# Spreading the first attention loads over the second sequence's projections, and hand-set program order through the last two attention units

## The chip, the cores and the metric

The kernel runs on one core of one Trainium2 chip. The metric is device time of one launch in microseconds (us); lower is better. The time of a kernel is the median of several runs. Engines are named as in the profile: PE is TensorE's matmul stream and PEld its weight loads, DVE is VectorE, ACT is ScalarE, POOL is GpSimd, and SP issues DMAs.

## What is computed

One transformer block in fp32, with layer norms behind each half. B=2 sequences of L=1024 tokens, D=512, 16 heads of 32. Cut to what matters:

```python
q = _split(lora_linear(x, Wq, bq, Bq, Aq))      # k and v alike
scores = jnp.einsum('bhqd,bhkd->bhqk', q, k) * SCALE
attn = jax.nn.softmax(scores, axis=-1)
out = jnp.einsum('bhqk,bhkd->bhqd', attn, v)
x = _layernorm(x + lora_linear(out, Wo, bo, Bo, Ao))
# FFN: 8 experts with 256 places each, top-1 routing, H=704
eidx = jnp.argmax(softmax(xt @ Wg), -1)          # tokens are dispatched to experts
h = silu(xd @ W1) * (xd @ W3);  oe = h @ W2
shared = silu(xt @ sw1) * (xt @ sw3) @ sw2
x = _layernorm(x + gate * oe[slot] + shared)
```

## The kernel before

**Precision.** Every large operand is split into a high and a low part (xh and xl, wh and wl, at_h and at_l, w13s's two halves), and a product takes three matmuls: high by high, low by high, high by low.

**Phase 1, projections (to L386).** Tokens go in four blocks tb of 512; tb 0 and 1 are the first sequence, tb 2 and 3 the second. For each block proj_qk (L290) runs eight times (four groups g of four heads, for q and for k), 12 matmuls each (L288) into one PSUM bank. store_qk (L298) then writes the high part oh on ACT (L303) and the low part ol on DVE (L304) into SBUF tiles of which there are two each, and SP stores both to DRAM (L305, L306; 256 KB each). Next come four proj_v (L308; L314 on PE, L319 on DVE, a store to vd at L321). The x tiles of the next block are loaded (L267) and split (xh on ACT L273, xl on DVE L274) meanwhile. During tb 3 a matmul stream for the first attention units is interleaved (pre_s1, L173): it finds row maxima (DVE, L181). Attention reads q, k and v back from DRAM in another layout: load_k (L130) is 3 DMAs of 512 KB, load_q (L152) 3 of 256 KB, load_v (L140) one of 512 KB. The loads for units 0 to 2 are issued in two blocks: k(0), q(0), q(1), k(1), q(2) after tb 1, and v(0) to v(3) after tb 2 (L378 to L386). In phase 1 only PE keeps the program's order; the order on ACT, DVE and SP is chosen by the tile scheduler. In the trace each of SP's DMAs waits for the one issued eight earlier to have landed: the store issued at 89.19 us waited for the qs load issued at 82.72, which landed at 89.13. mh and ml (L194 to L197) are the row maxima of a unit, stored as extra rows of its q tile.

**Phase 2, attention (from L543).** 16 units u (a sequence, four heads, 512 queries), eight steps of 128 keys each, 128 steps t in all. In a step, st_step (L555) makes four score matmuls (L566), each followed by an exponential on ACT (L575) that writes half of a tile pt; av_step (L590) makes the four value matmuls of the step before (L596). The softmax denominator is made by adding the pt tiles of a unit's steps (add_step, L578, the adds at L585) in two pairs pr of heads; the tables ON_DVE and DVE_END say which adds (step, pair) run on DVE, all others run on POOL. finish (L610) sums the result over partitions by matmuls with ones into sm (L619). The last step of a unit is not added but summed by four more of these matmuls (DIRECT), except in the units listed in NO_DIR. For units below RDIR=14 the inverse takes a way through DRAM (sd, r, invert at L640 with the reciprocal at L643, rd, and rb at L647); for units 14 and 15 it is one DVE reciprocal, rc (L629). normalize (L652) multiplies by the inverse (av, L658) and writes at_h on ACT (L660) and at_l on DVE (L662). oproj (L673) is the output projection of 128 tokens: 12 matmuls (L687), the residual add on DVE (L692), norm statistics (L529 to L532), the root on POOL (L538, L540) and the normalised row on ACT (L544). I write op10 to op17 for those of the second sequence. op10 is a generator of four times three matmuls that the loop advances once a step from step t = 128 + OPROJ1 on; what is left runs after the loop.

**What sets the order.** In the loop (L707 to L755) all engines keep the program's order (MAN2) until t = 112 (MAN_END); there steps.close() hands ACT, DVE, POOL and SP back to the scheduler, and only PE stays in program order.

**The tail (L756 on).** After the loop: op11 to op13, the router's setup (L418), and then the list TAIL in PE's order: normalize(15) ("n"), the splits of the shared expert's weight chunks w13 (s0 to s5: high on ACT at L509, low on POOL at L515, loads w13r on SP into two buffers at L501), transposes (p, L411, with xth on ACT L414 and xtl on DVE L415), op14 to op17 (o), logits (a, L464). Then follow the shared expert (L810), routing, dispatch and the experts.

Of the kernel before, what the change touches and what calls it, by code (L numbers as in the profile page):

```python
# [10 lines left out]
F32R = mybir.dt.float32r  # L11
# [7 lines left out]
P = 128  # L19
B, L, D = 2, 1024, 512  # L20
NU = 16
T = B * L
NH, HD = 16, 32
NG = 4
# [11 lines left out]
WARM, WCOL = 4, 256  # L36
OPER = 4
PTB = 13
MAN1 = {mybir.EngineType.PE}
MAN2 = {  # L40
    mybir.EngineType.PE, mybir.EngineType.Activation, mybir.EngineType.DVE,
# [2 lines left out]
MAN3 = {mybir.EngineType.PE}  # L44
MAN4 = MAN2 - MAN3
DIRECT = (7,)
MAN_END = 14 * 8
NO_DIR = (NU - 2, NU - 1)
FIN = 3
REC = 4  # L50
XTB = 5
# [11 lines left out]
FINE, NRME = 2, 4  # L63
DVE_END = {
    NU - 2: ((1, 0), (2, 1), (4, 1), (5, 1), (6, 0), (6, 1), (7, 0), (7, 1)),
    NU - 1: ((1, 0), (2, 0), (3, 0), (4, 0), (5, 0), (6, 0), (6, 1), (7, 0)),
}
OPROJ1 = -4
ROOT_LAG, NORM_LAG = 1, 4
HSB = 8  # L70
TAIL = "n s0 s1 s2 p0 o4 o5 s3 p1 o6 s4 o7 a0 s5".split()
# [12 lines left out]
def kernel(  # L84
# [48 lines left out]
    def load_k(g):  # L133
        kt = Ks[g % 2]
        for blk, hl in ((0, 0), (1, 1), (2, 0)):
            sp.dma_start(
                out=f(kt[32 * blk : 32 * blk + 32]),
                in_=qk_d[1, g // NG, g % NG, hl].rearrange("(h p) t -> p h t", p=32),
            )

    def load_v(g):
        if g < NG:
            vts[g] = x1b[:, :, g * P : g * P + P]
        else:
            vts[g] = mp_.tile([P, 8, P], F32, name=f"vt{g}", tag="vt", bufs=2)
        sp.dma_start(
            out=vts[g],
            in_=v_d[g // NG].rearrange("(c p) d -> p c d", p=P)[
                :, :, (g % NG) * P : (g % NG) * P + P
            ],  # L150
        )

    def load_q(u):
        g, qb = u // 2, u % 2
        for blk, hl in ((0, 0), (1, 0), (2, 1)):
            sp.dma_start(
                out=f(Qs[u % 3][32 * blk : 32 * blk + 32]),
                in_=qk_d[0, g // NG, g % NG, hl].rearrange("(h p) t -> p h t", p=32)[
                    :, :, qb * 512 : qb * 512 + 512
                ],  # L160
            )
# [42 lines left out]
    with ExitStack() as ph1, tc.manual_schedule(engines=MAN1):  # L204
        wp = ph1.enter_context(tc.tile_pool(name="wp", bufs=1, side="right"))
        sg = ph1.enter_context(tc.tile_pool(name="sg", bufs=2, side="right"))
# [83 lines left out]
        def proj_qk(tb, xs, w, g):  # L290
            o = bank1(f"o{tb}{w}{g}")
            for k in range(KC):
                proj_k(o, xs, w, g, k)
                if k % 2:
                    pre_s1(tb)
            store_qk(tb, w, g, o)

        def store_qk(tb, w, g, o):  # L298
            b, c0 = tb // 2, (tb % 2) * 512
            bias = bqk_sb[:, w * 4 + g : w * 4 + g + 1]  # L300
            oh = sg.tile([P, 512], F32R, name=f"oh{tb}{w}{g}", tag="oh")
            ol = sg.tile([P, 512], F32R, name=f"ol{tb}{w}{g}", tag="ol")
            act.activation(oh, o, AF.Identity, bias=bias)  # L303
            dve.scalar_tensor_tensor(ol, o, bias, f(oh), ALU.add, ALU.subtract)  # L304
            sp.dma_start(out=qk_d[w, b, g, 0][:, c0 : c0 + 512], in_=f(oh))  # L305
            sp.dma_start(out=qk_d[w, b, g, 1][:, c0 : c0 + 512], in_=f(ol))  # L306
# [46 lines left out]
        for tb in range(4):  # L353
            if tb == 0:
                for g in range(NG):
                    store_qk(0, 0, g, os_[g])
                    if g == 1:
                        sp.dma_start(out=bv_bc, in_=bvo[0:1, :].partition_broadcast(P))
                        r2 = load_w(2)
                for g in range(NG):  # L360
                    proj_qk(tb, xs, 1, g)
                    if g == 1:
                        prep_w(2, r2)
            else:
                for g in range(NG):
                    for w in range(2):
                        proj_qk(tb, xs, w, g)
            if tb < 3:
                xr = load_x(tb + 1)
            for t4 in range(4):  # L370
                proj_v(tb, xs, t4)
                if t4 == 1 and tb < 3:
                    xn = split_x(tb + 1, xr)
            if tb == 0:
                sp.dma_start(out=bo_bc, in_=bvo[1:2, :].partition_broadcast(P))
                prep_w(3, load_w(3))
            xs = xn
            if tb == 2:  # L378
                for g in range(NG):
                    load_v(g)  # L380
            if tb == 1:
                load_k(0)
                load_q(0)
                load_q(1)
                load_k(1)
                load_q(2)  # L386

    po, rt, xts = {}, {}, {}
    turn3 = cycle(range(4))
# [157 lines left out]
    with ph2, tc.manual_schedule(engines={mybir.EngineType.PE}):  # L547
# [60 lines left out]
        def direct(u):  # L608
            return () if u in NO_DIR else DIRECT

        fin = {}

        def finish(u):
            sm = one.tile([P, 512], F32, name=f"sm{u}", tag="one")
            parts = [lambda h, k_=k_: pts[u * 8 + k_, h // 2][:, h % 2, :] for k_ in direct(u)]
            parts.append(lambda h: accs[u, h // 2][:, h % 2, :])
            for i, pf in enumerate(parts):
                for h in range(4):
                    pe.matmul(  # L619
                        sm[32 * h : 32 * h + 32, :],  # L620
                        ones32,
                        pf(h),
                        start=i == 0,
                        stop=i == len(parts) - 1,
                        skip_group_check=True,
                    )
            if u >= RDIR:
                rc = ap.tile([P, 512], F32, name=f"rc{u}", tag="rc", bufs=1)
                dve.reciprocal(rc, sm)  # L629
                fin[u] = rc  # L630
                return
            rc = ap.tile([P, 512], F32, name=f"rc{u}", tag="rc", bufs=1)
            act.copy(rc, sm)
            sd = dram.tile([4, 512], F32, name=f"sd{u}")
            sp.dma_start(out=sd, in_=rc[0:P:32, :])
            r16 = ap.tile([P, 16], F32, name=f"r16_{u}", tag="r16", bufs=1)
            sp.dma_start(out=r16, in_=sd.rearrange("h (j c) -> (h j) c", c=16))
            fin[u] = r16
# [62 lines left out]
        def run(gen):  # L701
            for _ in gen:
                pass

        op10 = oproj(1, 0, 3)
        steps = ExitStack()
        steps.enter_context(tc.manual_schedule(engines=MAN2))  # L707
        for t in range(NS):
            u, k = t // 8, t % 8
            if t == MAN_END:  # L710
                steps.close()
            if k == 0:
                if u % 2 == 0 and 2 <= u and u // 2 + 1 < B * NG:
                    load_k(u // 2 + 1)
                if u >= 1 and u + 2 < NU:
                    load_q(u + 2)
                if u % 2 and NG <= u // 2 + 1 < B * NG:
                    load_v(u // 2 + 1)
            if t in RES_AT:
                load_res(RES_AT.index(t))  # L720
            between = [[], [], [], []]
            if early(t, 0):
                between[2].append(lambda: add_step(t, 0))
            if t + LEAD < NS:
                for q in range(4):
                    between[q].append(lambda q=q: s1_step(t + LEAD, q))
            elif t + LEAD == NS:
                between[0].append(lambda: finish_max(NU - 1))
            if t:
                between[1].append(lambda: av_step(t - 1))  # L730
                if u and k == (FINE if u == NU - 1 else FIN):
                    between[1].append(lambda: finish(u - 1))
            if u:
                if k == 7 and u < NU - 1:
                    between[0].append(lambda: normalize(u - 1, (0,)))
                    between[1].append(lambda: normalize(u - 1, (1,)))
                    between[2].append(lambda: normalize(u - 1, (2,)))
            if t - RES_ADD in RES_AT:
                between[3].append(lambda: add_res(RES_AT.index(t - RES_ADD)))
            st_step(t, between)  # L740
            if k == REC and 1 <= u < NU - 1:
                invert(u - 1)
            if u == NU - 1 and k == NRME:
                normalize(u - 1)
            if t in OPROJ_AT:
                op0 = oproj(0, OPROJ_AT.index(t), OPER)
            if OPROJ_AT[0] <= t:
                next(op0, None)
            if t + 1 in OPROJ_AT[1:]:
                run(op0)  # L750
            for _, fn in [x for x in later if x[0] == 0]:
                fn()
            later[:] = [(n - 1, fn) for n, fn in later if n]
            if t - NS >= OPROJ1:
                next(op10, None)  # L755
        av_step(NS - 1)  # L756
        finish(NU - 1)
        run(op10)
        for i in range(1, 4):
            run(oproj(1, i))  # L760
# [420 lines left out]
```

## Time and profile before

| | us |
|---|---|
| median of 3 runs (lowest, highest) | 1099.57 (1096.62, 1100.72) |
| the profiled execution | 1099.78 |
| span inside that execution | 1098.1 |
| PE busy | 1042.4 (95%) |
| DVE busy | 752.1 (68%) |
| POOL busy | 564.8 (51%) |
| ACT busy | 529.4 (48%) |
| mean granted PE clock | 0.987 |

A row of the profile has the line of the kernel, the engine, the operation, output<-input by the program's names, and times from the span's start. "Waits" rows give the time that an engine stood idle in front of an operation, with what came last before it could go. "Windows" rows give busy time and number of instructions of PE, PEld, DVE, ACT and POOL in a stretch, then the granted PE clock as a share of full speed, the busy share of the DMA engines, and GB/s. Stages in this execution: tb 2 starts at about 80 us, tb 3's first matmul at 122.91, unit 0's first scores at 166.89, op11 at 648.56, the first shared-expert matmul at 672.78.

### The profile page before, as it was taken

Reading aid. Unit: us, or ns where it says so; the run is one execution under the profiler, and the core shown is the slowest. Engines: PE = TensorE matmul, PEld = TensorE weight load, DVE = VectorE, ACT = ScalarE, POOL = GpSimd, SP = SyncE. Lnnn points to the kernel's source line nnn. Section 1 sums busy time; section 2 is a strip of 40 time slices with the busy share of each in tenths; the row PEclk is TensorE's granted clock in tenths of the full one; section 3 lists DMA queues with packets and bytes.
Section 4 is the critical chain, followed back from the end, with each engine's and each line's share of the span. In section 5 each row is a group of like instructions: output and inputs, shape, how many; then the busy total and the mean of one; then the engine's idle time right before and its main releaser. Section 6 shows DMA issues by size and latency. Waiting matters only on the chain.

```text
span 1098.1 us, 16442 instructions
## 1 busy us (share of the span) xinstructions
PE 1042.4 (95%) x5984; PEld 746.7 (68%) x5984; DVE 752.1 (68%) x1218; ACT 529.4 (48%) x1025; POOL 564.8 (51%) x380
## 2 busy tenths in 40 slices
PE   8997998999999999999999798999999999999995
PEld 6886884444444455544444257989999999999993
DVE  7642589899999987889998764333532557777752
ACT  5322115666666655566665545322222456555552
POOL 4000006888888877868898456000050036655555
PEclk9998999999999999999999989999999999999998
DMA  8879730141414242042520113000073356777532
GB/s 279 260 237 270 237 116 30 42 107 48 106 48 103 70 106 68 22 100 67 115 75 17 49 39 111 35 10 20 26 233 108 117 188 230 238 248 245 185 97 76
DMA packets 77585, 131.24 MB, mean 120 GB/s; under 512 B 14344, under 2 KB 23048, under 8 KB 77504
## 3 DMA queue, kind: packets, MB, share of 16 engines
q1 hardware_dynamic: 73664, 117.59, 36.8%
q0 software_dynamic: 3840, 12.60, 3.2%
q8 instruction: 47, 0.77, 0.3%
q14 instruction: 34, 0.28, 0.1%
HBM read 96.10 MB, written 33.80 MB: 118 GB/s over the span
## 4 chain that ended last, share of the span: by engine, by line
PE 57%; DVE 24%; DMA 7%; ACT 5%; issue 3%; POOL 3%; SPq 1%; POOLq 0%; DVEq 0%; ACTq 0%
DVE mt L181 11%; DVE pt L585 7%; PE av L596 7%; PE st L566 6%; PE s L173 6%; PE h L810 6%; PE o L288 5%; PE v L314 4%; PE y L854 3%; DMA qkd<-oh 2%; PE op L687 2%; DMA be<-bs_d,meta 1%; DVE w13s L515 1%; ACT w2s L797 1%; ACT w13s L509 1%
## 5 line engine op out<-in xcount | busy, mean ns | idle before, releaser
L585 POOL TENSOR_TENSOR pt<-pt,pt 128x1024 f32<-128x1024 f32 x152 | 360.0, 2392 | 232.2 <-ACT pt L575 215.4
L181 DVE TENSOR_REDUCE mt<-s 128x1 f32<-128x512 f32 x512 | 323.5, 681 | 38.0 <-PE s L173 37.7
L575 ACT ACTIVATE pt<-st 128x512 f32<-128x512 f32 x512 | 271.1, 602 | 151.6 <-PE st L566 149.4
L566 PE MATMUL st<-qs,ks 98*128 98x512 f32 x512 | 216.9, 434 | 1.2 <-ACT pt L575 1.2
L173 PE MATMUL s<-ks,qs 96*128 96x512 f32 x512 | 202.6, 403 | 12.6 <-DVE mt L181 11.5
L566 PEld LDWEIGHTS st<-qs,ks 98*128 98x128 f32 x512 | 96.6, 191 | 136.6 <-issue 88.0
L810 PE MATMUL h<-xthe,w13s 128*128 128x256 f32 x704 | 129.9, 283 | 0.0
L173 PEld LDWEIGHTS s<-ks,qs 96*128 96x128 f32 x512 | 97.0, 189 | 41.4 <-DVE mt L181 26.9
L798 POOL TENSOR_TENSOR w2s<-w2r,w2s 128x512 fp32r<-128x512 f32 x48 | 69.2, 1458 | 95.3 <-ACT w2s L797 94.1
L810 PEld LDWEIGHTS h<-xthe,w13s 128*128 128x128 f32 x704 | 110.7, 191 | 0.3
L585 DVE TENSOR_TENSOR pt<-pt,pt 128x1024 f32<-128x1024 f32 x44 | 92.9, 2120 | 14.4 <-ACT pt L575 12.1
L810 PE MATMUL h<-xtle,w13s 128*128 128x256 f32 x352 | 100.2, 285 | 2.2 <-DVE xtle L415 2.2
L596 PE MATMUL av<-pt,vt 128*32 128x512 f32 x512 | 74.2, 619 | 2.9 <-DVE at_l L662 2.9
L810 PEld LDWEIGHTS h<-xtle,w13s 128*128 128x128 f32 x352 | 67.4, 191 | 3.6 <-DVE xtle L415 3.0
L854 PE MATMUL y<-w2s,hs 128*128 128x512 f32 x272 | 65.6, 398 | 3.7 <-POOL w2s L798 3.7
L596 PE MATMUL av<-pt,x1b 128*32 128x512 f32 x512 | 68.2, 605 | 0.0
L958 POOL DMA_INDIRECT xd_d<-x1a,slot_i x8 | 8.0, 994 | 112.1 <-DVE slot_i L955 109.9
L854 PEld LDWEIGHTS y<-w2s,hs 128*128 128x128 f32 x272 | 51.4, 192 | 15.3 <-POOL w2s L798 5.0
L288 PE MATMUL o<-xh,wh 128*128 128x512 f32 x128 | 52.3, 409 | 8.2 <-DVE ol L304 6.4
L303 ACT ACTIVATE oh<-o,bqk_sb 128x512 fp32r<-128x512 f32 x32 | 22.0, 688 | 65.6 <-PE o L288 34.8
L288 PE MATMUL o<-xh,wl 128*128 128x512 f32 x128 | 51.9, 405 | 0.0
L288 PE MATMUL o<-xl,wh 128*128 128x512 f32 x128 | 51.8, 404 | 0.0
(807 smaller groups left out, 1747.7 us busy)
## 6 DMA issues: line engine op xcount, KB each, us to landing
qs<-qkd SPq DMA_DIRECT2D x48, 256.0 KB, 7.1
ks<-qkd SPq DMA_DIRECT2D x24, 512.0 KB, 7.0
w2r<-in_w_dram SPq DMA_DIRECT2D x48, 256.0 KB, 3.3
x1a<-in_w_dram SPq DMA_DIRECT2D x24, 512.0 KB, 6.8
qkd<-oh SPq DMA_DIRECT2D x32, 256.0 KB, 3.1
qkd<-ol SPq DMA_DIRECT2D x32, 256.0 KB, 2.2
x1b<-in_w_dram SPq DMA_DIRECT2D x16, 512.0 KB, 6.8
x1b<-in_wT_dram SPq DMA_DIRECT2D x16, 256.0 KB, 5.4
```

Source lines behind the costliest of these rows:

```text
L173: pe.matmul(s1, Qs[u % 3][0:96, h, qt * P : qt * P + P], Ks[g % 2][0:96, h, kh * 512 : kh * 512 + 512], start=True, stop=True,)
L181: dve.tensor_reduce(mts[u][:, c, kh : kh + 1], s1, AX.X, ALU.max)
L288: pe.matmul(o, lhs, rhs, start=k + i == 0, stop=k + i == KC + 1)
L303: act.activation(oh, o, AF.Identity, bias=bias)
L314: pe.matmul(o, lhs, rhs[:, k, :], start=n == 0, stop=n == 11)
L566: pe.matmul(sb, Ks[g % 2][:, h, kc * P : kc * P + P], Qs[u % 3][:, h, :], start=True, stop=True,)
L575: act.activation(pts[t, h // 2][:, h % 2, :], sb, AF.Exp, scale=SCALE)
L585: eng.tensor_tensor(accs[u, pr], accs[u, pr], pts[t, pr], ALU.add)
L596: pe.matmul(avs[u][32 * h : 32 * h + 32, :], vts[g][:, kc, 32 * h : 32 * h + 32], pts[t, h // 2][:, h % 2, :], start=kc == 0, stop=kc == 7 ...
L798: pool.tensor_tensor(hl[:, 1, :], raw, f(hl[:, 0, :]), ALU.subtract)
L810: pe.matmul(hp[:, j * 256 : j * 256 + 256], lhs, rhs[:, k, :], start=n == 0, stop=n == 11,)
L854: pe.matmul(o, lhs, rhs, start=n == 0, stop=n == 16)
```

## The change

Five edits. (a) The oh and ol tiles get three buffers in place of two. (b) The two blocks of loads are removed; a table LOADS says after which group g of which block tb each load is issued in the program: k(0), q(0), q(1) in tb 2, v(0), k(1), q(2) and v(1) to v(3) in tb 3. (c) steps.close() moves from t = 112 to behind finish(15), so ACT, DVE, POOL and SP keep program order in units 14 and 15 too. (d) Unit 15 leaves NO_DIR: its last step is summed by four more matmuls, and the adds (7,0) on DVE and (7,1) on POOL are gone. (e) OPROJ1 goes from -4 to -2: op10's first matmuls come after step 126, and six of its 12 after the loop.

In the compiled order of the changed kernel k(0) and two parts of q(0) stand ahead of tb 2's stores in SP's queue, as part of them did before. In tb 2 the queue holds four pairs of stores (oh, ol), the third part of q(0), four more pairs, q(1), and the four x loads of tb 3. Behind them come the v stores with v(0), k(1) in parts among tb 3's pairs, q(2), and v(1) to v(3) ahead of unit 0's mh and ml.

```diff
+OHB = 3
+LOADS = {
+    (2, 0): (("k", 0),), (2, 1): (("q", 0),), (2, 3): (("q", 1),),
+    (3, 0): (("v", 0),), (3, 1): (("k", 1),), (3, 2): (("q", 2),),
+    (3, 3): (("v", 1), ("v", 2), ("v", 3)),
+}
...
-MAN_END = 14 * 8
-NO_DIR = (NU - 2, NU - 1)
+NO_DIR = (NU - 2,)
...
-    NU - 1: ((1, 0), (2, 0), (3, 0), (4, 0), (5, 0), (6, 0), (6, 1), (7, 0)),
+    NU - 1: ((1, 0), (2, 0), (3, 0), (4, 0), (5, 0), (6, 0), (6, 1)),
 }
-OPROJ1 = -4
+OPROJ1 = -2
...
-            oh = sg.tile([P, 512], F32R, name=f"oh{tb}{w}{g}", tag="oh")
-            ol = sg.tile([P, 512], F32R, name=f"ol{tb}{w}{g}", tag="ol")
+            oh = sg.tile([P, 512], F32R, name=f"oh{tb}{w}{g}", tag="oh", bufs=OHB)
+            ol = sg.tile([P, 512], F32R, name=f"ol{tb}{w}{g}", tag="ol", bufs=OHB)
...
                     for w in range(2):
                         proj_qk(tb, xs, w, g)
+                    for fn, a_ in LOADS.get((tb, g), ()):
+                        {"k": load_k, "q": load_q, "v": load_v}[fn](a_)
...
-            if tb == 2:
-                for g in range(NG):
-                    load_v(g)
-            if tb == 1:
-                load_k(0)
-                load_q(0)
-                load_q(1)
-                load_k(1)
-                load_q(2)
...
-            if t == MAN_END:
-                steps.close()
...
         finish(NU - 1)
+        steps.close()
         run(op10)
```

## The prediction

> **What bounds the kernel now.** I read the page first: the share of each engine, then the granted clock by slices.
>
> ```profile
> PE 1042.4 (95%) x5984; PEld 746.7 (68%) x5984; DVE 752.1 (68%) x1218; ACT 529.4 (48%) x1025; POOL 564.8 (51%) x380
> ...
> PEclk9998999999999999999999989999999999999998
> ```
>
> TensorE (PE) is busy 95% of the span, so time can only come from its gaps and from stretches at a lower clock. After the start, the clock row dips in two inner slices of 27.45 us: the fourth (82 to 110 us) and the twenty-fourth (631 to 659 us). The change touches both places. The list of waits names one long PE wait for each:
>
> ```profile
> PE o L288 <- DVE ol L304: 6.4, 1, 6.4
> DVE xl L274 <- ACT xh L273: 6.0, 6, 2.8
> PE op L687 <- DVE at_l L662: 5.9, 1, 5.9
> ```
>
> (Total, times, longest.) The chain of waits between 80 and 123 us shows what is behind the first:
>
> ```profile
> 82.72 6.41 DMA qs<-qkd
> 89.19 12.56 DMA qkd<-oh
> 101.86 0.70 ACT oh L303
> 102.58 0.76 DVE ol L304
> 103.39 8.64 PE o L288 x24
> 112.03 10.88 PE v L314 x48
> 122.91 1.37 PE o L288 x6
> ```
>
> (Start, length, what.) A 256 KB store of oh took 12.56 us, since the block of loads after tb=1 stood ahead of it. With two oh buffers ACT couldn't write the next one, the PSUM banks stayed full, and PE stood from about 97 to 103.39. Then 24 matmuls took 8.64 us; at full speed (the 48 after them: 10.88/48 = 0.227 each) they take 5.44. The windows of both places give busy time and, after the five engines, the clock, DMA share and GB/s:
>
> ```profile
> 98.00:104.00 6.00, 0.61 (x2) 0.53 (x3) 0.93 (x2) 1.38 (x2) 0.00 (x0) 0.61 0.95 311
> 104.00:110.00 6.00, 6.00 (x16) 4.75 (x15) 3.83 (x6) 3.30 (x5) 0.00 (x0) 0.53 0.99 336
> ...
> 612.00:615.00 3.00, 0.07 (x2) 0.01 (x1) 1.39 (x2) 2.12 (x5) 0.00 (x0) 0.97 0.94 293
> 615.00:622.00 7.00, 7.00 (x35) 2.92 (x37) 3.38 (x2) 2.74 (x6) 2.37 (x1) 0.77 0.07 28
> ...
> 627.00:633.00 6.00, 0.26 (x1) 0.29 (x2) 5.59 (x4) 1.42 (x3) 3.56 (x2) 0.90 0.00 0
> 633.00:641.00 8.00, 8.00 (x30) 3.79 (x30) 1.59 (x2) 3.26 (x6) 1.87 (x1) 0.64 0.00 0
> ```
>
> PE waits, and then runs at part of its clock. The stall at 627 is made on DVE, whose order from step 112 the scheduler chose:
>
> ```profile
> 622.29 3.35 DVE L629 RECIPROCAL rc<-sm 128x512 f32<-128x512 f32 x1
> 625.56 3.15 DVE L585 TENSOR_TENSOR pt<-pt,pt 128x1024 f32<-128x1024 f32 x1
> 628.63 0.69 DVE L658 TENSOR_TENSOR av<-av,rc 128x512 f32<-128x512 f32 x1
> ```
>
> Two adds (3.15 and, at 629.23, 2.76) stand between rc and at_l(14), which ends 632.60, and op10's first matmuls wait for it.
>
> **Phase 1: spread loads, third oh/ol buffer.** tb=2 begins at about 80.5. Its 96+48 matmuls at 0.227 take 32.6 us, so tb=3 could begin at 113.1; it began at 122.91. The loss is 9.8, of which 6.4 is the wait and 3.2 the half clock. The block held back k0's last part, q0, q1, k1 and q2, some 4.1 MB. From 89.13 to 101.75 eight of its transfers (3.15 MB) went through, 249 GB/s. In the changed order only q0's third part follows tb=2's first four pairs of stores, q1 follows all eight, then come the four x loads. A pair (0.52 MB) per 2.72 us of matmuls is 193 GB/s, which the queue carried before (windows here show 215 to 336). So tb=2 runs without a wait.
>
> Next late: the x tiles of tb=3. The x loads stand behind q1 and leave at about 106 to 107; landing at 109.5 to 112, plus 0.62 for xh and 0.69 for xl, the tiles are ready from 111.1 to 113.5, and needed from 113.1 to 115.7: 2 us to spare, 0.8 at 215 GB/s. Then v0, k1, q2 share tb=3 with its stores: from 80 to 144 some 16.4 MB must move, 256 GB/s, which is near what the windows show, but the third buffer gives each store 2.7 us more. Last, unit 0's mh and ml now queue behind v1 to v3 (1.57 MB, 6.3 us at 249 GB/s): ml left at 156.98 and unit 0 needed it at 166.89, so of 7 us to spare 1.5 to 2 remain. I take the gain as **9.6** (6.4+3.2). Ends: 4 if x tiles and stores come late by 6, 10 if all hides.
>
> Here a rule speaks for less. The Trainium skill, "TensorE: Matmul & The Clock Gate", Part 1, holds that the clock halves after an idle window of about 3.4 us and returns after about 3.4 us of sustained work. An estimate by it: 1.7 us lost per restart, none after a gap under 3.4, so 6.4+1.7 = 8.1 here. The trace has 0.53 over 104 to 110, a loss of 3.2, and 0.77 after the gap of only 2.93 at 612. I use the rows.
>
> **Units 14 and 15: program order, unit 15's last sums, op10 two steps later.** From 590 to op11's start (648.56) PE loses: 2.93 at 612, where rb(13) came late; 7x0.23 = 1.6 of clock after it; 5.86 for at_l(14); 8x0.36 = 2.9 of clock; 0.89 for POOL's last add (645.17 to 647.53). Sum 14.2.
> - normalize(13): the reciprocal of r stood behind three DVE adds, at 607.62. r's load was issued at 599.65, 3.4 after sd's store; in a hand-ordered unit that took 1.72 (539.17 to 540.89). In program order the reciprocal runs at about 600.5, rb lands at 606.2, at_l(13) ends about 610.2, and PE asks at 612.1. The 2.93 and the 1.6 go.
> - at_l(14): it now follows rc at once. op10's matmuls start after step 126, by when it is done, so 5.86 and 2.9 go. New: ACT's at_h(14) stands in program order ahead of step 125's exponentials and waits for rc (3.35) and av; behind it wait the exponentials, and for them PE's scores. By the rows this costs 2.4 (ACT resumes at 626.3, not at 623.9). It is below every idle gap after which the trace shows a lower clock.
> - Unit 15's kc=7: 4 more sm matmuls (sm x4 takes 1.03) for one DVE add (1.1 alone) and POOL's 2.36. PE +1.0, and the 0.89 goes. op10's 12 matmuls are moved, not multiplied.
> - SP's queue in these units holds only r, rd and rb; their DMAs (each about 2 us) are hidden above. POOL's adds keep to their units, and ones that met DVE's were stretched (2.37 to 2.94), which is in these rows.
>
> 14.2-2.4-1.0, less 0.7 for exponentials that PE meets sooner: op11 starts at 638.5, **10 us** earlier.
>
> **What of these 10 reaches the end.** In the listing of the changed order ACT's at_h(15) comes after the high parts of w13 chunks 2 and 3 and the normalised rows op10 to op12 (before: right after the gate weights, at 653.52). The last row needs POOL's root behind chunk 3's low part. From POOL's start at 638.1: low part 2.36, load 3.6, high 1.0, low 2.36, two roots 1.8, low 2.36, root 0.9, row 0.75, at_h 0.56, at_l 0.66 = 16.4, so op14 starts at 654.6 (before 657.82). But PE has finished op10 to op13 by 647.7: it idles 7 us, and by the row of the 5.86 gap loses about 3 more to the clock (by the skill's rule 1.7). That leaves 3.2-3 = 0.2 at op17. Then two waits go, as ACT gets there sooner: 1.9 for xtls before the first shared matmul (672.78) and 1.93 at 684.25 before lg. Sum 0.2+3.8 = **4.0**; 7 without the clock loss, 0 if both waits return. Beyond that PE is nearly gapless, so a shift stays.
>
> **Sum.** 9.6+4.0 = 13.6, against the profiled execution's 1099.78 (span 1098.1), which is the median 1099.57 within 0.02%: 1086.
>
> **Rivals.**
> - *Loads collide again* (x tiles behind q1, mh behind v1 to v3). For: 256 GB/s against 249 measured in the block. Against: 2 us to spare at each place. Phase 1 gives 4 to 6: 1090 to 1092.
> - *The tail gives nothing*: at_h(15) later than worked out, both waits back. Phase 1 alone: 1090.
> - *The tail keeps 7*: no clock loss, 1083; if op14 also starts sooner because rows and chunks interleave better on the chip, 1079 to 1081.
> - *It doesn't do what it says*: SP's order in phase 1 is the scheduler's. The listing shows the loads spread as named; I give this nothing.
> - *Slower*: the one mechanism is ACT's order around at_h(15). Each us that op14 starts later is one us at the end. With 9.6 won and 3.8 from the two waits less 3 for the clock, the balance is zero when op14 starts 10.4 later than before, at 668, and slower by 0.5% at 674. My chain says 654.6; the loads of w13 would have to take 3.6+13 us. No row shows that. Price then over 15 us: 1106.
>
> **Chances.** Forecast (1083 to 1089) 0.46; collision 0.15; tail nothing 0.15; tail full 0.10; both fail, within 0.5% (5.5 us, about what a measurement can tell from no change) 0.09; slower 0.05. Faster: 0.46+0.15+0.15+0.10 = 0.86, of which I move 0.03 to the other two, as the order of four engines is worked out by hand. Range 1079 to 1094: all faster cases but the edges.
>
> **What would show it.** The clock row's fourth slice at 9 or more; oh's wait for its store under 1 us each; tb=3's first matmul at 113 to 114 (right), 116 to 119 (collision). at_l's wait gone from op's list; op11 10 us sooner after step 112 than before; an idle PE of 5 to 9 us ahead of op14 (right), none (tail full), over 15 (slower). Wrong would also be a new wait of the first scores for ml, or PE waits for exponentials over 4 us at step 125.

## The result and the profile after

The changed kernel takes 1083.39 us (median of 4 runs, 1082.82 to 1084.25); the kernel before, run beside it, 1098.6 (1096.62 to 1100.72). The ratio is 0.9862 with a 95% interval of 0.9841 to 0.9883: 15.2 us faster, where 13.6 were forecast. The profiled execution took 1083.41 with a span of 1081.7, so the two profiled executions differ by 16.4.

The page of the changed kernel, the same rows as before (engine totals, and the granted clock by slices):

```profile
PE 1041.9 (96%) x5992; PEld 746.5 (69%) x5992; DVE 749.2 (69%) x1217; ACT 528.6 (49%) x1025; POOL 564.6 (52%) x379
...
PEclk8999999999999999999999999999999999999997
```

PE works as long as before (1041.9 us against 1042.4), and the two inner dips of the clock row are gone. In PE's list of waits (total, times, longest) both long waits are gone too:

```profile
PE s L178 <- DVE mt L186: 11.1, 19, 2.2
PE y L851 <- POOL w2s L795: 3.2, 2, 1.7
PE o L293 <- ACT wh L267: 2.6, 1, 2.6
PE st L564 <- ACT pt L573: 2.5, 5, 1.3
PE op L685 <- ACT at_h L658: 2.2, 1, 2.2
```

The row of at_h is new: op14 waits for unit 15's at_h, once, 2.2 us. The chain of waits through tb 2 and into tb 3 (start, length, what):

```profile
80.64 21.77 PE o L293 x96
102.43 0.70 ACT oh L308
103.16 0.76 DVE ol L309
104.31 4.78 DMA qs<-qkd
109.15 6.16 DMA vd<-x1a
115.38 1.27 DVE x1a L324 x2
116.65 0.61 DVE mt L186
117.30 0.51 PE s L178
```

The 96 matmuls of tb 2 run in one piece, 21.77/96 = 0.227 each. What is late next stands below them: the store of a v tile waited behind q(1) and the x loads and landed at 115.3, DVE's next bias add (x1a) waited for it, then the row maxima, then PE. That chain costs PE only 0.31 us at 117.30. The windows of both places (busy PE, PEld, DVE, ACT, POOL, then the clock, DMA share, GB/s):

```profile
98.00:104.00 6.00, 6.00 (x28) 4.99 (x27) 1.97 (x3) 1.38 (x2) 0.00 (x0) 1.00 0.47 177
104.00:110.00 6.00, 6.00 (x28) 4.95 (x28) 1.38 (x2) 0.00 (x0) 0.00 (x0) 1.00 0.94 218
...
640.00:645.00 5.00, 3.11 (x18) 2.37 (x16) 1.39 (x2) 2.51 (x4) 3.79 (x5) 1.00 0.47 136
645.00:650.00 5.00, 4.41 (x11) 3.32 (x12) 3.64 (x9) 2.75 (x5) 2.69 (x2) 0.66 0.65 227
```

98 to 110 is full at full clock, where before there was a 6 us hole. The gap that remains lies in the tail, ahead of op14 (PE is busy 3.11 of 5 us), with a lower clock behind it (0.66).

To see where the time came from, I read the start of the same event in each trace. The table has the shift against the profiled execution of before, in us, counted from the start of tb 2, since the start-up ahead of it varies by up to 0.8 between executions. "Unit 0" is its first score matmul, "sd(0)" and "sd(13)" the stores of those units' sums, "h" the first matmul of the fifth shared-expert tile, and "end" the span.

| kernel | tb 3 | unit 0 | sd(0) | sd(13) | op11 | op17 | h | end |
|---|---|---|---|---|---|---|---|---|
| changed | -9.7 | -8.5 | -6.4 | -6.6 | -16.9 | -12.5 | -16.4 | -16.4 |
| p1_both | -9.7 | -8.8 | -6.7 | -6.8 | -6.8 | -6.8 | -4.5 | -5.6 |
| p1_buf | -8.2 | -8.2 | -5.6 | -5.7 | -7.1 | -7.1 | -4.8 | -6.3 |
| p1_loads | -8.3 | -6.3 | -4.7 | -4.9 | -5.7 | -5.7 | -4.7 | -4.2 |
| tail_all | 0.2 | 0.2 | 1.5 | 1.2 | -9.2 | -6.2 | -10.0 | -10.4 |
| tail_order | -1.6 | -1.6 | -0.1 | -0.4 | -2.8 | -1.3 | -0.3 | 0.0 |
| tail_sums | -1.3 | -1.3 | 0.2 | 0.1 | -7.9 | -2.8 | -6.7 | -5.9 |
| after_op4 | -9.7 | -8.4 | -6.4 | -6.6 | -13.2 | -13.1 | -10.3 | -9.8 |
| norm_first | -9.7 | -8.7 | -6.5 | -6.7 | -17.1 | -17.2 | -19.0 | -20.0 |

The versions other than the changed kernel are described in the next section. tail_order and tail_sums have phase 1 of before and still start tb 3 1.3 to 1.6 sooner: that is how far one execution is from another, and the account of phase 1 below shows where it comes from.

### The profile page after: what moved, and what is told of

The parts are those of the page before. It is cut to its first block, busy times and chain, and to the rows that moved or that the text cites. A ratio compares the mean times of both kernels' runs of the same rounds, so it can differ in the third digit from the quotient of the medians.

```text
span 1081.7 us, 16449 instructions
## 1 busy us (share of the span) xinstructions
PE 1041.9 (96%) x5992; PEld 746.5 (69%) x5992; DVE 749.2 (69%) x1217; ACT 528.6 (49%) x1025; POOL 564.6 (52%) x379
## 4 chain that ended last, share of the span: by engine, by line
PE 68%; DVE 21%; DMA 3%; ACT 3%; POOL 2%; issue 2%; SPq 0%; POOLq 0%; DVEq 0%; ACTq 0%
DVE mt L186 10%; PE o L293 8%; PE h L807 8%; PE av L594 8%; PE st L564 7%; DVE pt L583 7%; PE s L178 7%; PE y L851 4%; PE v L319 3%; PE op L685 3%; DMA be<-bs_d,meta 1%; DVE av L656 1%; POOL w2s L795 1%; DVE w13s L513 1%; ACT w13s L507 1%
## 5 line engine op out<-in xcount | busy, mean ns | idle before, releaser
L178 PE MATMUL s<-ks,qs 96*128 96x512 f32 x512 | 203.2, 404 | 12.5 <-DVE mt L186 11.1
L583 DVE TENSOR_TENSOR pt<-pt,pt 128x1024 f32<-128x1024 f32 x43 | 90.6, 2112 | 3.4 <-ACT pt L573 2.8
L851 PEld LDWEIGHTS y<-w2s,hs 128*128 128x128 f32 x272 | 52.0, 195 | 15.2 <-POOL w2s L795 4.8
```

Source lines behind the costliest of these rows:

```text
L178: pe.matmul(s1, Qs[u % 3][0:96, h, qt * P : qt * P + P], Ks[g % 2][0:96, h, kh * 512 : kh * 512 + 512], start=True, stop=True,)
L583: eng.tensor_tensor(accs[u, pr], accs[u, pr], pts[t, pr], ALU.add)
L851: pe.matmul(o, lhs, rhs, start=n == 0, stop=n == 16)
```

## The experiments

**The halves.** p1_both is the kernel before with edits (a) and (b), p1_buf with (a) alone, p1_loads with (b) alone, tail_all with (c), (d) and (e). Gains are worked out from the ratios, at some 1099 us.

> The kernel before with the loads spread and the third oh/ol buffer, and nothing of the attention edits. My theory (the trace of the changed kernel: tb 3 starts 9.6 us sooner, unit 0 8.5 us sooner): faster by 8 to 9.6 us, tb 3's first matmul at about 113.1, unit 0's first scores at about 158.4. Rival (the loads collide again and the rest of the gain is the tail's): faster by 4 to 6 us.

Measured: 1093.58 us, ratio 0.9945 (0.9927 to 0.9962), so 6.0 faster: the rival's number, but not its cause. tb 3 starts 9.7 sooner and unit 0 8.8 sooner, as I had it; nothing collides. The gain is lost later: 2.1 in unit 0 (below) and some 2 in the shared expert, where ACT reads the logits tile ls late and PE now waits for it once for 3.2 us, in place of 1.53 and 1.93 in two waits before. The two waits of before, then the windows of p1_both around its one:

```profile
672.56 0.39 PE L810 MATMUL h-1_0_0_6511<-xths,w13s-1_0_6310 128*128 128x256 f32 x1 [1.53 <-DVE xtls L415]
684.25 0.29 PE L464 MATMUL lg<-xths,wgr 128*16 128x256 f32 x1 [1.93 <-DVE xtls L415]
...
665.00:670.00 5.00, 1.80 (x14) 1.59 (x13) 3.85 (x10) 1.88 (x3) 2.25 (x6) 0.89 0.10 38
670.00:675.00 5.00, 5.00 (x25) 5.00 (x25) 0.85 (x2) 4.75 (x8) 1.87 (x3) 0.50 0.00 0
```

One wait of 3.2 us is followed by half the clock for 5 us (25 matmuls where a full window of this stage has about 43); the two waits of before left it at 1.00. Why the waits fall differently there is not shown.

> The kernel before with the third oh/ol buffer alone; the loads stay in their two blocks. My theory (the block of loads is the cause, a buffer only puts the stall off by one tile of 2.7 us): faster by 2.7 to 4.5 us, PE still stands 3 to 4 us near 100. Rival (two buffers are the cause): faster by 8 us or more, no PE wait near 100.

Measured: 1093.16 us, ratio 0.9946 (0.9933 to 0.9959), 5.9 faster. My theory fell: tb 3 starts 8.2 sooner with the loads where they were. ACT in p1_buf (start, length, operation, then the idle time before it) shows the block still in the way, and PE's one wait there:

```profile
100.37 0.69 ACT L304 ACTIVATE oh<-o,bqk_sb 128x512 fp32r<-128x512 f32 x1 [11.25 <-DMA qkd<-oh]
103.14 0.50 PE L315 MATMUL v<-wh,xh 128*128 128x512 f32 x1 [1.15 <-DVE ol L305]
```

ACT waits 11.25 us for a store in place of 15.07, but PE waits only 1.15 us, after tb 2's 96 matmuls (at 103.14): the banks and three tiles carry it through nearly the whole burst, and a gap so short cost no clock (1.00 in both windows from 98 to 110).

> The kernel before with the loads spread, two oh/ol buffers as before. My theory: a store lands in 2 to 3 us and a tile comes every 2.7 us, so two buffers are enough in tb 2 and the gain is nearly whole, 7.5 to 9.6 us. Rival (the third buffer is needed for the stores behind the loads in tb 3): 4 to 7 us, with ACT waits for stores of 1 us or more in tb 3.

Measured: 1094.6 us, ratio 0.9954 (0.994 to 0.9968), 5.1 faster. tb 3 starts 8.3 sooner, unit 0 only 6.3. The gain is the rival's, but its sign did not come: ACT waits for no store from 80 to 165 us. PE waits for tb 3's x tiles:

```profile
113.61 0.50 PE L293 MATMUL o<-xh,wh 128*128 128x512 f32 x1 [1.16 <-ACT xh L278]
114.34 0.50 PE L293 MATMUL o<-xl,wh 128*128 128x512 f32 x1 [0.23 <-DVE xl L279]
```

The x loads leave 27.9 us after tb 2's start (25.3 in the changed kernel), because the scheduler here puts DVE's bias add at 104.33 ahead of the last two ol, which then run at 104.94 and hold up the stores in front of the loads. Either edit alone takes most of the stall away; together they add 1.4 to that at tb 3. The three totals lie within each other's intervals.

> The kernel before with program order in units 14 and 15, unit 15's last step summed by matmuls, and op10 two steps later; phase 1 as before. My theory (stage by stage from the two traces: 16.4 less 8.5): faster by 6.5 to 8 us, op11 8 to 9 us sooner. By the prediction's sum: 4 us. Rival (the tail takes all back): within 2 us of before.

Measured: 1089.23 us, ratio 0.9901 (0.9886 to 0.9916), 10.9 faster: more than my theory's 8 and far more than the prediction's 4. From sd(13) to op11 it gains 10.4, and from op11 to the end loses nothing (-9.2 to -10.4). With p1_both's 6.0 the halves make 17 against 15.2 measured together; the intervals (about 1.6 to 2.3 us each way) cover that.

**The parts of the tail.** tail_order is (c) alone, tail_sums (d) and (e) alone; after_op4 is the changed kernel with one line changed back:

```diff
-OPROJ1 = -2
+OPROJ1 = -4
```

> The kernel before with program order in units 14 and 15 alone; op10's matmuls still start after step 124 and unit 15's last step is still added. My theory: the waits for rb(13) go (2.9 us and 1.6 of clock), but op10's first matmuls now stand for at_l(14), which follows rc(14) by about 6 us, so 3 to 5 us of PE wait remain and ACT's program order adds its own: faster by 2 to 5 us. Rival (order is the whole of it): faster by 6.5 to 8 us.

Measured: 1100.25 us, ratio 1.0006 (0.9996 to 1.0016): no gain, less than I expected. op11 comes 2.4 sooner than sd(13)'s shift; 0.9 of that is left at op17 and nothing at h. PE's waits in tail_order from 615 to 650 us:

```profile
PE op L687 <- DVE at_l L662: 4.6, 1, 4.6
PE sm L619 <- POOL pt L585: 2.0, 1, 2.0
PE sm L619 <- DVE pt L585: 1.7, 1, 1.7
```

As long as op10 asks for at_l(14) at step 124, PE's wait for it only shrinks from 5.86 to 4.58, and for unit 15's last adds, which (d) removes, PE waits 3.7 in place of 0.89.

> The kernel before with op10 two steps later and unit 15's last step summed by matmuls; units 14 and 15 stay with the scheduler. My theory: PE no longer asks for at_l(14) at step 124, so most of 5.9 us and 2.9 of clock go, the wait for rb(13) stays: faster by 3 to 6 us. Rival (a late at_l(14) only meets PE two steps later): faster by under 2 us.

Measured: 1093.51 us, ratio 0.994 (0.9924 to 0.9956), 6.6 faster (5.8 by the medians), at the upper end of my theory. So the two table edits carry over half of the tail's gain alone, order alone nothing, and both 10.9: order pays only once op10 and the sums are out of its way.

> The changed kernel with op10's first matmuls again after step 124 (OPROJ1 = -4). My theory: PE waits there for at_l(14), 4 to 6 us, less the 1.35 that it waits for exponentials anyway: slower than the changed kernel by 3 to 6 us (1086 to 1089). Rival (in program order at_l(14) is in time): within 1 us of the changed kernel.

Measured: 1089.52 us, ratio to before 0.9925 (0.9898 to 0.9952), against the changed kernel's 0.9862: 6 to 7 slower, the upper end of what I expected or just above it. PE waits 4.6 us for at_l(14), and later 4.2 for ls.

**A version beyond the change, and two more causes.** norm_first moves normalize(15) ahead of the hand-back, so that its DVE and ACT steps follow rc(15):

```diff
         finish(NU - 1)
+        normalize(NU - 1)
         steps.close()
...
-TAIL = "n s0 s1 s2 p0 o4 o5 s3 p1 o6 s4 o7 a0 s5".split()
+TAIL = "s0 s1 s2 p0 o4 o5 s3 p1 o6 s4 o7 a0 s5".split()
```

> The changed kernel with normalize(15) ahead of the point where the order is handed back, so its three steps follow rc(15) in program order and do not wait behind the w13 parts and rows. My theory: at_l(15) is ready near 636 instead of 646, op14 runs without a gap, so the 2.5 us of wait and 1.7 of clock go: faster than the changed kernel by 3.5 to 4.5 us, about 1079. Rival (the next thing is late at once, POOL's chain of w13 low parts and roots holds op14 to op17's rows or the first shared matmuls): 0 to 1.5 us faster. A third view, that no clock is lost after so short a gap: 2.5 us.

Measured: 1081.18 us (1079.26 to 1088.06), ratio to before 0.9843 (0.9819 to 0.9868). The gap ahead of op14 and its half clock are gone, op17 comes 4.7 sooner than in the changed kernel; then 1.5 us of wait for ls return and 2.6 remain at h. Since the interval overlaps that of the changed kernel, I ran both on one chip:

> The changed kernel, unaltered, to stand beside the three versions of this group on one chip. Every theory: about 1083.4 us, as measured first (1082.8 to 1084.3).

> The version with normalize(15) ahead of the hand-back, once more, beside the changed kernel. My theory: its gap ahead of op14 (2.5 us) and the clock loss behind it (1.7) are gone, of which 1.5 came back as a wait for ACT's ls in the shared expert: 2 to 4 us faster than the changed kernel. Rival (the first measurement's gain of 2.1 us was chance): within 1 us.

Measured: the changed kernel 1094.12 (1091.09 to 1096.89), norm_again 1093.66 (1090.11 to 1098.81), before 1110.14 on that chip; ratios 0.9864 (0.9844 to 0.9884) and 0.9862 (0.9837 to 0.9886). My expectation of 2 to 4 us isn't borne out by the times, though that trace again has norm_again 2.5 ahead between sd(13) and h. The rival (within 1 us) holds: that it is faster stays unproven. The changed kernel's ratio came out as at first.

unit0_pool and loads_late are built on norm_first:

```diff
 DVE_END = {
+    0: (),
```

> As the one before, and unit 0's two adds (1,0) and (2,1) run on POOL in place of DVE. My theory: DVE's add beside POOL's (3.30 us) is what PE's 2.15 us wait for the row maxima in unit 0 comes from, and the half clock after it costs another 1.3 to 2: 2 to 4 us faster. If no clock is lost behind a gap so short: 2. Rival (POOL with 12 adds of 2.4 us in a unit of 28 us becomes the late one, and sm(0) waits): same or slower by 1 to 3 us.

Measured: 1098.72 us, ratio 0.9908 (0.989 to 0.9925), so 5 slower than norm_again: the rival, though by another way than it named. The first wait is gone, but POOL runs unit 0's twelve adds back to back (28.12 us from 163.28) and comes to its first pause at 194.92; DVE's add of unit 1 lies beside that and ends at 196.01:

```profile
188.19 7.82 DVE L584 TENSOR_TENSOR pt<-pt,pt 128x1024 f32<-128x1024 f32 x1
```

An add that takes 1.2 us alone takes 7.82, and PE waits 6.83 us for the maxima behind it.

```diff
-    (2, 0): (("k", 0),), (2, 1): (("q", 0),), (2, 3): (("q", 1),),
-    (3, 0): (("v", 0),), (3, 1): (("k", 1),), (3, 2): (("q", 2),),
+    (2, 0): (("k", 0),), (2, 1): (("q", 0),),
+    (3, 0): (("q", 1),), (3, 1): (("k", 1),), (3, 2): (("v", 0), ("q", 2)),
```

> As the version with normalize(15) early, with q(1) behind the x loads and v(0) with q(2), so that the v stores of tb 2 wait for fewer loads. My theory: DVE's adds of bv no longer wait 6 us for a v store, the waits of 0.3 and 0.7 us at both ends of tb 3 go: 0.7 to 1.2 us faster. Rival (the slack was there, and q(1) or unit 0's maxima now come late): same or slower by 1 us or more.

Measured: 1095.16 us, ratio 0.9873 (0.9852 to 0.9895), the same as norm_again within the intervals. PE's waits of this kernel from 150 to 215 us:

```profile
PE st L564 <- DMA qs<-ml: 3.2, 1, 3.2
PE s L178 <- DVE mt L186: 2.8, 3, 2.2
```

The waits at both ends of tb 3 are gone, as I meant, and unit 0's first scores wait 3.2 us for ml behind the loads instead: the rival. The place is the one that the prediction had left with 1.5 to 2 us to spare.

## Why the prediction was right, point by point

The time and the range held, but two terms of the sum were off by 3.2 and 5.5, in opposite directions: phase 1 brought 6.4 in place of 9.6, units 14 and 15 and the tail 9.8 in place of 4.0 (in the two traces). That the sum came within 1.6 us is in part luck.

**Phase 1, 9.6: right at its place, 6.4 at the end of unit 0.** tb 3's first matmul started at 113.11 (113 to 114 was to show it right), 9.6 sooner (it started at 122.75 before; the chain's row gives 122.91). Its clock part, 3.2, is what one execution had. Windows of before (first two lines) and of tail_order (last two), which has the same phase 1 and the same wait of 6.4 us:

```profile
102.79:106.20 3.41, 2.81 (x7) 2.26 (x8) 2.42 (x4) 2.00 (x3) 0.00 (x0) 0.50 0.86 319
106.20:109.62 3.42, 3.42 (x10) 2.68 (x9) 1.76 (x3) 2.00 (x3) 0.00 (x0) 0.50 0.99 320
...
102.20:105.61 3.41, 3.06 (x7) 2.48 (x8) 2.43 (x4) 2.16 (x4) 0.00 (x0) 0.50 0.89 318
105.61:109.02 3.41, 3.41 (x16) 2.78 (x16) 1.68 (x4) 1.83 (x3) 0.00 (x0) 1.00 0.97 328
```

In before PE ran 6.2 us at half clock and lost 3.1; in tail_order 3.1 us, and lost 1.5. So against an execution like tail_order's the change gains about 8 at tb 3, near the 8.1 that the prediction had put aside.

The term failed in that the prediction let this shift stay. 1.2 was lost in tb 3. The prediction had looked at x tiles and at mh and ml as next late; the x tiles cost 0.3, and what it had not looked at, the v stores behind the loads, made DVE late for all of tb 3 (0.31 at its start and 0.70 us at its end). Another 2.1 went in unit 0. There PE waits about 2.17 us for a row maximum in both kernels, because DVE's add lies beside POOL's (3.30 us). In before (first two lines) the clock stays full behind that wait; in tail_all (last two), which has the same phase 1, it does not:

```profile
181.30:184.71 3.41, 2.04 (x13) 0.77 (x13) 3.29 (x6) 0.08 (x1) 2.55 (x2) 1.00 0.00 0
184.71:188.12 3.41, 3.41 (x18) 1.50 (x17) 2.67 (x5) 2.33 (x6) 3.41 (x2) 1.00 0.04 10
...
181.19:184.61 3.42, 1.71 (x10) 0.63 (x11) 3.39 (x6) 0.25 (x1) 2.22 (x1) 1.00 0.00 0
184.61:188.02 3.41, 3.41 (x9) 1.99 (x8) 2.51 (x5) 2.35 (x5) 3.41 (x3) 0.50 0.04 10
```

So 1.3 to 1.5 of the 2.1 (the same loss in tail_all, tail_order and tail_sums) is no effect of the change: the profiled execution of before had escaped a loss that its siblings have. after_again escaped it too, and there unit 0 loses 0.6; what makes that rest stays open.

**Units 14 and 15, 10: right.** From sd(13) to op11 the trace gains 10.3. The waits of 2.93, 5.86 and 0.89 are gone. The changed kernel at the end of unit 14:

```profile
613.41 5.22 DVE L583 TENSOR_TENSOR pt<-pt,pt 128x1024 f32<-128x1024 f32 x2
619.89 0.69 DVE L660 TENSOR_TENSOR at_l<-av,at_h 128x512 fp32r<-128x512 f32 x1 [0.65 <-ACT at_h L658]
620.41 0.50 PE L564 MATMUL st<-qs,ks 98*128 98x512 f32 x1 [1.35 <-ACT pt L573]
623.43 0.40 PE L685 MATMUL op<-wo_h,at_h 128*128 128x512 f32 x1
```

ACT's new stall behind at_h(14) costs PE 1.35 where 2.4 was taken, and no clock. (That even 2.4 would cost none is not safe: in unit 0 of the changed kernel a wait of 2.17 us was followed by 3.41 us at half clock.) One thing was not as described: at_l(14) doesn't follow rc at once, two adds (5.22 us together) stand between them in program order as well. It still ends at 620.58, ahead of op10's first matmul at 623.43, because that asks two steps later; without (e), after_op4 loses 6 to 7, and it is one of the two reasons why tail_order gains nothing.

**The tail, a loss of 6: it lost 0.5.** The time of at_l(15) was right within 2 us: 654.6 less the 6.6 by which sd(13) is sooner is 648.0, and op14's first matmul with it started at 646.09. The failed step is "so op14 starts at 654.6", with 7 us of idle PE. PE in the changed kernel:

```profile
642.71 0.40 PE L685 MATMUL op<-wo_l,at_h 128*128 128x512 f32 x1
645.36 0.50 PE L685 MATMUL op<-wo_h,at_h 128*128 128x512 f32 x1 [2.25 <-ACT at_h L658]
646.09 0.50 PE L685 MATMUL op<-wo_h,at_l 128*128 128x512 f32 x1 [0.23 <-DVE at_l L660]
```

The first nine of op14's 12 matmuls read head groups of older units and ran before the wait; I had held all 12 for the last group. From op13's end (640.15) to 646.09 passed 5.9 us; in them PE ran transposes (0.6), those nine (2.3) and a tenth (0.5). So PE idled 2.25+0.23, not 7 (5 to 9 was to show it right: that sign failed), and the clock cost (1-0.66)x5 = 1.7, not 3. The two waits after it went, as forecast; the first was 1.53 in the trace, where the sum had 1.9.

**The rivals.** "The tail keeps 7" named 1083, which is nearer to the 1083.39 measured than the forecast's 1086, but not by its way: 1.7 of clock were lost there, and phase 1 brought less. Nothing collided in the change as made, though loads_late shows how near it was. "The tail gives nothing" was wrong, and so was the slower case: op14's wait was a third of what I had feared.

## What to carry to other kernels

A stall that a burst of loads makes can be taken away by moving the burst or by one more buffer, and either may do most of it; so test them apart before crediting one. Follow a gain to the end of the program, since a shifted stage meets its next waits in another combination: two short waits that become one long one can cost a stretch of half clock. Before a loss of clock is put into a sum, see whether other executions of the same stage have it. When a matmul group waits for its last operand, count the matmuls of the group that need only older data; they run first and shorten the gap.

## What the hardware showed that I had not expected

The clock's answer to a gap is not fixed by its length. After a wait of 2.17 us in before's unit 0 it stayed at 1.00, after 2.15 in the same place of tail_all it fell to 0.50; a wait of 1.93 cost nothing in before, and one of 1.94 in tail_order was followed by half clock. What decides is where the gap lies. In all fourteen traces the granted clock is, from 15 us on, either 1.00 or 0.50, and it changes only on a raster of 3.41 us, which lies elsewhere in each execution; the windows under phase 1 above are laid on it. Full clock gave way to half after every raster stretch in which PE was idle 1.72 us or more, after none with 1.39 or less, and after some between. Half clock ended after each stretch with at most 0.43 us idle and after none with 0.44 or more. Before's wait in unit 0 was cut by the raster at 181.30 (0.80 and 1.37 us); tail_all's had 1.70 in one stretch. So such a gap costs nothing or whole raster stretches at half clock, 1.7 us each where PE works through them: one behind the 2.48 us ahead of op14, two behind p1_both's 3.2.

The Trainium skill, "TensorE: Matmul & The Clock Gate", Part 1, says that the activity window of about 3.4 us runs free of the program, so that its phase decides, and these traces agree; but it names an idle window, and here a window half idle was enough, so the measurement decides.

The chip of the last four kernels was 1% slower for all of them, before included. after_again stands at h with no delay against the changed kernel's first trace, and its span is 7.7 longer; its trace shows a run of PE gaps of 0.3 to 1.1 us between 792 and 802 us that wait for nothing that the profile shows, with a clock of 0.62 over 800 to 810. The three other traces of that chip have such gaps at 791 to 810 us, the ten before none. What makes them stays open.
